# Four seams of a four-layer kernel: squares and projection by image in layer 0, a LayerNorm by token rows in layer 2, and the start and end of layer 3's attention

## The chip, the cores and the metric

The kernel runs on one core of one Trainium2 chip. The metric is the device time of one execution in microseconds. Before the change it was 3514.43 us, the median of 3 runs (3514.23 to 3514.61).

The core has five engines that run their own instruction streams beside each other: TensorE (PE in the profile, its weight loads are PEld), VectorE (DVE), ScalarE (ACT), GpSimd (POOL) and SyncE (SP, which here only issues DMAs). A matrix product goes from SBUF to PSUM; the other engines bring it back.

## The reference

Four layers follow one another on x, four images of 256 channels and 32 x 32 places (B = 4, D = 256, L = 1024 tokens per image). Cut to what matters:

```
# layer 0: a state space layer (Mamba-2) and a squeeze-and-excite gate
u = layernorm(x over channels)
y = scan(u) * silu(z)
y = y * rsqrt(mean(y * y) + eps) * rms_w          # per token
out = y @ out_w.T
attn = sigmoid(relu(mean_over_tokens(out) @ se1_w.T + se1_b) @ se2_w.T + se2_b)
x = x + out * attn                                  # one gate per image and channel
# layer 1: a non-local block, theta, phi and g with one channel each
f = theta x phi / N;  y = f @ g
x = x + batchnorm(w * y + b)
# layer 2: attention and a mixture of 8 experts, top 2, on t = tokens of x
n = layernorm(t);  t = t + softmax(q(n) k(n) / 16) v(n)
t = t + moe(layernorm(t))
# layer 3: attention over channels and an LSTM
n = layernorm(t);  query, key = n @ W_qk + b_qk;  value = n @ W_v + b_v
lam = softmax(key over tokens).T @ value            # 256 x 256 per image
lam = batchnorm(lam over images and value channels) * gamma + beta
t = t + query @ lam
t = t + lstm(layernorm(t))                          # 1024 steps, in order
```

All of it is in fp32.

## The kernel before, in words

The activations stay in SBUF. `s.x` holds x with the channels on the partitions (two chunks of 128 channels, C = 2), `s.xr` holds token rows (128 tokens on the partitions, 32 such tiles, NT = 32, 8 per image). A block is 512 tokens (W), of which an image has two (BPI = 2). A planner orders instructions on each engine by their dependencies, the order in which they are written and the buffers of the tile pools; a pool with n buffers makes the n+1st user wait for the first to be done. Where `_in_order` is called, the order written is fixed for PE, DVE and ACT.

Layer 0 ends with `_scan` (L376 to L436) and `_out_and_se` (L439 to L493). The scan goes over 8 chunks of 128 tokens of 4 images, 32 in all. `_out_and_se` first takes the 32 Squares with a sum on ACT (L449), a Sqrt on ACT (L451) and a reciprocal (L452). Then it goes over the eight blocks: the rows are scaled on DVE (L459), turned by PE (`pt`, L463), copied with rms_w on DVE (`yT`, L464) and projected (`po`, L470); ACT copies the result to `o` with a sum over tokens (L473). After the last block come the mean, the two small products of the gate, the sigmoid (L491) and eight updates of x on DVE (L493).

Layer 1 (`_layer1`, L499 to L612) reduces the block to sums: 64 matmuls (L535), one row of statistics, a chain of small DVE operations with `_rsqrt`, and then per image and channel chunk `theta` on PE (L602), `wy` on ACT (L607) and an addition to x on DVE (L612).

`_rsqrt` (L971 to L994) is a Newton iteration on DVE with four rounds; it is a generator, so that its operations can be placed beside other work.

Layer 2 begins with `_layernorm` (L184 to L216) for all eight blocks: the mean over channels by a matmul with a matrix of averages (L196), a subtraction on DVE (L197), Square on ACT (L199), the variance by a matmul (L201), and after the last block Sqrt (L209), reciprocal (L211), a broadcast by matmuls from eight rows (`wide`, L215) and the multiplication (L216). `_layer2_attention` (L712) then goes over the images: q (L743), v (L755), scores (L768) for eight groups of 128 queries with softmax between, the transposes of the probabilities (L792) and the product with v (L804). `beside(n)` takes n parts of a generator between these steps; for images 1 to 3 the parts are those of `_head` (the LayerNorm, gate and scatter for the experts) for the image before, for image 0 there are none. The experts follow; they scatter their results to DRAM from POOL's queue.

Layer 3's attention (`_layer3_attention`, L1247 to L1398) loads y, the two expert results of each token, by 16 DMAs from SP's queue (L1282), adds the two on POOL (L1285) and the sum to the token rows on DVE (L1287), takes statistics per tile of 128 tokens (L1291, L1292), then `_rsqrt` for the image's eight tiles, the normalised rows on ACT (L1302) and transposes (L1268, `p_x`) with copies on DVE (L1273). Keys (L1318), their softmax over tokens, and `lam` follow per image. After the last image comes the batch norm over all images (`_batchnorm`, L615, with a Sqrt on ACT, L625, and L1377, L1378). The query weights are folded into lam: `lam_q` by 16 matmuls (`p_q`, L1384), and the query bias by 32 (`p_b`, L1394) into `add_col`.

Layer 3's LSTM (`_layer3_lstm`) loads its weights on ACT's DMA queue, makes its constants (bias, `fold`, `mask`, `shift`, L1429 to L1443) and then `ahead(0)`: the attention output of the first 128 tokens of each image is added to x (`attended`, L1464 and L1458) and their input gates are computed (`input_gates`). The loop of 1024 steps takes one part of `ahead(n + 1)` per step beside its own chain: `hidden` on PE (L1616), transposes on DVE (L1645), activations on ACT (L1646, L1659), the new hidden state on DVE (L1661). The loop's order is fixed by `_in_order`.

Of the kernel before, what the change touches and what calls it, by code (L numbers as in the profile page):

```python
# [18 lines left out]
P = 128  # L19
B = 4  # L20
# [46 lines left out]
NW = {"w_l0": 260 + 512 + 256 + 64, "w_l2": 768 + 8, "w_l3": 768, "w_u": 768, "w_v": 768}  # L67
# [91 lines left out]
def _in_order(s, start):  # L159


    engines = mybir.EngineType
    before = {}
    for i in s.nc.cur_bb.bb.instructions[start:]:
        if i.engine not in (engines.PE, engines.DVE, engines.Activation):
            continue
# [17 lines left out]
def _layernorm(s, u):  # L184

    nc = s.nc
    with ExitStack() as ctx:
        pool = ctx.enter_context(s.tc.tile_pool(name="ln", bufs=2))
        ps = ctx.enter_context(s.tc.tile_pool(name="ln_ps", bufs=2, space=PSUM))
        ps1 = ctx.enter_context(s.tc.tile_pool(name="ln_ps1", bufs=1, space=PSUM))  # L190
        var = ps1.tile([NBLK, W], F32, name="var")
        for i in range(NBLK):
            t = bass.ts(i, W)
            mean = ps.tile([P, W], F32, name="mean")
            for k in range(C):
                nc.tensor.matmul(mean, s.avg, s.xt[:, k, t], start=k == 0, stop=k == C - 1)  # L196
            nc.vector.tensor_sub(u[:, :, t], s.xt[:, :, t], _bc(mean, 1, C))  # L197
            sq = pool.tile([P, C, W], F32, name="sq")
            nc.scalar.activation(sq, u[:, :, t], AF.Square)  # L199
            for k in range(C):  # L200
                nc.tensor.matmul(  # L201
                    var,
                    s.avg_row[:, NBLK - 1 - i : 2 * NBLK - 1 - i],
                    sq[:, k, :],
                    start=i == 0 and k == 0,
                    stop=i == NBLK - 1 and k == C - 1,
                )
        std = pool.tile([NBLK, W], F32, name="std", bufs=1)
        nc.scalar.activation(std, var, AF.Sqrt, bias=s.eps[:NBLK])  # L209
        rstd = pool.tile([NBLK, W], F32, name="rstd", bufs=1)  # L210
        nc.vector.reciprocal(rstd, std)  # L211
        for i in range(NBLK):
            t = bass.ts(i, W)
# [117 lines left out]
def _decays(s, keep, dtr):  # L331
# [41 lines left out]
    return dt, (a, head), total, tail  # L373


def _scan(s, xbc, zs, dt, decay, total, tail):  # L376

    nc, tc = s.nc, s.tc
    a, head = decay
# [1384 lines left out]
```

## Time and profile before

| What | Value |
|---|---|
| Runs | 3514.23 to 3514.61 us, median 3514.43 |
| Profiled execution | 3514.67 us |
| Its span | 3512.7 us (1.97 us lie around it) |
| Mean granted TensorE clock | 0.969 |
| PE, DVE, ACT, POOL busy in the span | 92%, 57%, 35%, 12% |
| Layer 0 to the end of the scan | 0 to 295.4 us |
| Projection and gate | to 358.9 us |
| Layer 1, first to last `theta` and x | to 394.6 us |
| LayerNorm of layer 2 | 393.4 to 442.4 us |
| Attention of layer 2, images 0 to 3 | from 442.4, 527.4, 615.2 and 701.9 us |
| Last scatter of the experts | issued at 1386.6 us |
| Attention of layer 3 | PE from 1423.0 to 1528.6 us |
| LSTM with its first inputs | from 1547 us to the end |

How to read the profile's lines: times are in us from the start of the span, L12 is line 12 of the kernel. A timeline line has the start, the duration of a run of equal instructions, the engine, the line, the operation, "out<-in" by the program's names, the shape and the count, and in brackets the time that the engine had been idle before it and what ended the idle time. The chain that ended last is followed back from the last instruction, at each step to what released it; "issue" there is time in which an engine waited for nothing that the profile shows. PEclk is the clock that TensorE was granted, 1.00 or a 9 in the slices for full speed. PE's ends are modelled, since its matmuls are pipelined.

### The profile page before, as it was taken

Reading aid. Unit: us, or ns where it says so; the run is one execution under the profiler, and the core shown is the slowest. Engines: PE = TensorE matmul, PEld = TensorE weight load, DVE = VectorE, ACT = ScalarE, POOL = GpSimd, SP = SyncE. Lnnn points to the kernel's source line nnn. Section 1 sums busy time; section 2 is a strip of 40 time slices with the busy share of each in tenths; the row PEclk is TensorE's granted clock in tenths of the full one; section 3 lists DMA queues with packets and bytes.
Section 4 is the critical chain, followed back from the end, with each engine's and each line's share of the span. In section 5 each row is a group of like instructions: output and inputs, shape, how many; then the busy total and the mean of one; then the engine's idle time right before and its main releaser. Section 6 shows DMA issues by size and latency. Waiting matters only on the chain.

```text
span 3512.7 us, 146893 instructions
## 1 busy us (share of the span) xinstructions
PE 3227.6 (92%) x65412; PEld 2536.4 (72%) x65412; DVE 2016.5 (57%) x8382; ACT 1245.0 (35%) x5047; POOL 416.3 (12%) x498
## 2 busy tenths in 40 slices
PE   7786899998999997789999999999999999999888
PEld 4464344447788886468888888888888888888776
DVE  5795534452211111747777776777777777767666
ACT  4623222223222222413334344343343343433333
POOL 0182001122433332100000000000000000000000
PEclk9898899999999999899999999999999999999999
DMA  1290001115556554100000000000000000000000
GB/s 67 80 303 5 9 0 37 37 50 197 195 189 219 208 190 165 60 2 4 4 11 4 5 10 4 4 10 4 6 9 5 10 4 5 10 4 5 10 4 10
DMA packets 79355, 189.31 MB, mean 54 GB/s; under 512 B 6592, under 2 KB 64256, under 8 KB 73728
## 3 DMA queue, kind: packets, MB, share of 16 engines
q0 software_dynamic: 16176, 116.06, 9.0%
q1 hardware_dynamic: 60624, 59.12, 5.7%
q8 instruction: 511, 8.37, 1.0%
q10 hardware_dynamic: 1920, 4.74, 0.4%
q14 instruction: 124, 1.02, 0.1%
HBM read 118.88 MB, written 61.02 MB: 51 GB/s over the span
## 4 chain that ended last, share of the span: by engine, by line
PE 41%; DVE 9%; ACT 4%; issue 2%; ACTq 0%; DVEq 0%
PE p_c L1616 11%; DVE turned L1645 7%; PE p_c L1607 7%; PE p_i L1607 4%; PE p_o L1607 4%; PE p_i L1616 4%; PE p_o L1616 4%; PE beside L1560 4%; ACT a_o L1646 2%; DVE x L1661 2%; ACT th L1659 2%; PE beside L1464 1%; PE beside L1501 0%; PE var L1511 0%; PE p_q L1384 0%
## 5 line engine op out<-in xcount | busy, mean ns | idle before, releaser
L1646 ACT ACTIVATE add<-turned 128x8 f32<-128x8 f32 x1024 | 214.3, 209 | 1027.5 <-DVE turned L1645 1027.5
L1616 PE MATMUL p_c<-w_v,x 128*4 128x64 f32 x16368 | 416.0, 219 | 72.8 <-DVE x L1661 71.0
L1607 PE MATMUL p_c<-xg,shift 128*128 128x64 f32 x2048 | 445.7, 299 | 0.0
L1616 PE MATMUL p_o<-w_v,x 128*4 128x64 f32 x16368 | 416.6, 219 | 0.1
L1616 PE MATMUL p_i<-w_v,x 128*4 128x64 f32 x16368 | 416.5, 219 | 0.0
L1607 PE MATMUL p_i<-xg,shift 128*128 128x64 f32 x2048 | 406.8, 280 | 0.0
L1645 DVE STREAM_TRANSPOSE turned<-p_c 128x64 f32<-128x64 f32 x1024 | 255.9, 250 | 257.1 <-PE p_c L1616 226.7
L1607 PE MATMUL p_o<-xg,shift 128*128 128x64 f32 x2048 | 396.0, 275 | 0.0
L1607 PEld LDWEIGHTS p_c<-xg,shift 128*128 128x128 f32 x2048 | 304.7, 188 | 117.6 <-issue 0.3
L1616 PEld LDWEIGHTS p_c<-w_v,x 128*4 128x4 f32 x16368 | 227.2, 85 | 196.3 <-DVE x L1661 121.2
L1661 DVE TENSOR_TENSOR x<-a_o,th 128x8 f32<-128x8 f32 x1024 | 171.9, 168 | 245.4 <-ACT th L1659 245.4
L1607 PEld LDWEIGHTS p_o<-xg,shift 128*128 128x128 f32 x2048 | 310.9, 192 | 0.3
L1607 PEld LDWEIGHTS p_i<-xg,shift 128*128 128x128 f32 x2048 | 304.8, 188 | 0.4 <-issue 0.3
L1187 PE MATMUL ph<-uT,w 128*128 128x256 f32 x1248 | 284.6, 386 | 20.8 <-DVE uT L1172 20.7
L1191 ACT ACTIVATE hT<-ph,w 128x256 f32<-128x256 f32 x312 | 147.9, 474 | 395.2 <-PE ph L1187 394.8
L1187 PEld LDWEIGHTS ph<-uT,w 128*128 128x128 f32 x1248 | 240.4, 194 | 58.2 <-DVE uT L1172 24.6
L1201 PE MATMUL po<-w,hT 128*128 128x256 f32 x1248 | 282.1, 379 | 0.0
L1616 PEld LDWEIGHTS p_o<-w_v,x 128*4 128x4 f32 x16368 | 281.2, 87 | 0.3 <-issue 0.3
L1616 PEld LDWEIGHTS p_i<-w_v,x 128*4 128x4 f32 x16368 | 281.2, 87 | 0.3
L1645 DVE STREAM_TRANSPOSE turned<-p_i 128x64 f32<-128x64 f32 x1024 | 271.6, 265 | 0.7 <-PE p_i L1607 0.3
L1645 DVE STREAM_TRANSPOSE turned<-p_o 128x64 f32<-128x64 f32 x1024 | 256.0, 250 | 0.3 <-PE p_o L1616 0.3
L1201 PEld LDWEIGHTS po<-w,hT 128*128 128x128 f32 x1248 | 234.0, 190 | 30.2
(437 smaller groups left out, 4395.4 us busy)
## 6 DMA issues: line engine op xcount, KB each, us to landing
sorted<-zeros SPq DMA_DIRECT2D x32, 1032.0 KB, 14.4
y_in<-results SPq DMA_DIRECT2D x16, 512.0 KB, 5.3
x<-in_x_dram SPq DMA_DIRECT2D x8, 512.0 KB, 8.7
tokens<-rows SPq DMA_DIRECT2D x4, 1024.0 KB, 4.7
x<-tokens SPq DMA_DIRECT2D x8, 512.0 KB, 4.2
out_dram<-x_l SPq DMA_DIRECT2D x64, 64.0 KB, 1.7
results<-y,place POOLq DMA_INDIRECT x78, 4.4
w_l<-in_w_l_dram ACTq DMA_DIRECT2D x1, 1092.0 KB, 11.4
```

Source lines behind the costliest of these rows:

```text
L1187: nc.tensor.matmul(ph, w1[:, k, bass.ts(n, P)], uT[:, k, :], start=k == 0, stop=k == C - 1,)
L1191: nc.scalar.activation(hT[:, n, :], ph, AF.Gelu, bias=b1[:, n : n + 1])
L1201: nc.tensor.matmul(po, hT[:, n, bass.ts(a, P)], w2[:, n, :], start=n == 0, stop=n == NHC - 1,)
L1464: nc.tensor.matmul(p, lam[:, k, b, bass.ts(m, P)], u_l3[:, k, b * L + n * SB : b * L + (n + 1) * SB], start=k == 0, stop=k == C - 1,)
L1560: nc.tensor.matmul(p[bass.ts(i, R), :], rows[:, k, bass.ts(g, R)], w_u[:, k, at : at + GQ // GC], start=k == 0, stop=k == C - 1, tile_posi ...
L1607: nc.tensor.matmul(p[:, :H], shift[:, row * B : row * B + P], xg[n][:, g, bass.ts(i, H)], start=True, stop=t == 0,)
L1616: nc.tensor.matmul(p[R * i : R * i + B, :H], hs[:, t - 1, bass.ts(k, B)], w_v[:, k, i * GQ + g * H : i * GQ + (g + 1) * H], start=False, s ...
L1645: nc.vector.transpose(zt.rearrange("p c w -> p (c w)"), pz[g][:, :H])
L1646: nc.scalar.activation(dst.rearrange("p (c b) -> p c b", c=C), zt[:, :, :B], f)
L1659: nc.scalar.activation(th, cell[:, :, 1], AF.Tanh)
L1661: nc.vector.tensor_mul(h, a_o, th)
```

## The change

Layer 0. Each chunk's Square goes into `_scan`, behind the chunk's last operation. `_out_and_se` takes 1/sqrt by `_rsqrt` on DVE, in two parts (28 columns and the last 4), so Sqrt and reciprocal go. It then goes over images, not blocks: scaling is shared by DVE and ACT, the copies out of the transposes are on ACT with the sums over tokens, rms_w is multiplied into the weights once (`wo`), the gate's means are taken from the projection's input (a product with the mean of the rows in place of the mean of the products), and the four products of an image stay in four PSUM banks until the gate of this image is there; PE's order within an image is written out. x is updated from PSUM, four operations per image.

Layers 1 and 2. `_layer1` is called from `_layer2_attention` between the loading of layer 2's weights and `_layer2_weights`. `_layernorm` is replaced by `_norm_parts` for one image: transposes of x to token rows, a copy on ACT and statistics on DVE, `_rsqrt`, the normalised rows on ACT, transposes back and copies on DVE. Image 0's parts are run in layer 1 after image 0's x is done, with DVE's order fixed from there to the end of image 1; those of images 1 to 3 are the parts beside image 0's attention. `theta` has one PSUM buffer and not two.

`_rsqrt` and the LSTM's copy of it have three rounds, not four.

Layer 3. The two y are added on DVE, one after the other, and POOL has none of it. Image 0 is normalised in two groups of 512 tokens, each with its own `_rsqrt`, in a fixed order; the additions of later images are held behind the last copy of image 0's normalised rows. The LSTM's constants and bias loads come ahead of the attention. The weight array has another 256 columns, the query weights in their other orientation: the queries of the first 128 tokens of each image are computed in the attention (`q`), so that the first block's output is `lam` times q, and folding the weights into `lam` (`queries`) becomes eight groups placed between the parts of `ahead(0)`. A Sqrt with no other use is put ahead of the batch norm, and the batch norm's two wide operations per chunk become one.

The diff, cut to its core:

```diff
-def _layernorm(s, u):
+def _norm_parts(s, pool, u, b, psum):
+    mv = pool.tile([P, TPI, 2], F32, name="mv")
+    rows = pool.tile([P, TPI, D], F32, name="rows")
+    for n in range(0, TPI, 2):
+        p = psum()
+        for i in range(2):
             for k in range(C):
+                at = i * D + k * P
+                nc.tensor.transpose(
+                    p[:, at : at + P], s.x[:, k, b, bass.ts(n + i, P)], s.ident
                 )
+        yield
+        nc.scalar.copy(rows[:, n : n + 2, :].rearrange("p n d -> p (n d)"), p)
+        stats = pool.tile([P, 2, nc.vector.BN_STATS_DIM], F32, name="stats")
+        for i in range(2):
+            nc.vector.bn_stats(stats[:, i, :], p[:, bass.ts(i, D)])
+        for i in range(2):
+            nc.vector.bn_aggr(mv[:, n + i, :], stats[:, i, :])
+        yield
+    rstd = pool.tile([P, TPI], F32, name="rstd")
+    for i, _ in enumerate(_rsqrt(s, pool, rstd, mv[:, :, 1])):
+        if i % 2:
+            yield
+    shift = pool.tile([P, TPI], F32, name="shift")
+    nc.vector.scalar_tensor_tensor(shift, mv[:, :, 0], -1.0, rstd, ALU.mult, ALU.mult)
+    yield
+    for n in range(TPI):
+        nc.scalar.activation(
+            rows[:, n, :], rows[:, n, :], AF.Identity,
+            bias=shift[:, n : n + 1], scale=rstd[:, n : n + 1],
+        )
+        if n % 4 == 3:
+            yield
+    for i in range(BPI):
+        for c in range(C):
+            p = psum()
+            for j in range(TPB):
+                nc.tensor.transpose(
+                    p[:, bass.ts(j, P)], rows[:, i * TPB + j, bass.ts(c, P)], s.ident
+                )
+            yield
+            nc.vector.tensor_copy(u[:, c, b * L + i * W : b * L + (i + 1) * W], p)
+            yield
...
 def _scan(s, xbc, zs, ss, dt, decay, total, tail):
...
+                sq = pool.tile([P, D], F32, name="sq")
+                nc.scalar.activation(sq, zs[:, n, :], AF.Square, accum_out=ss[:, c * B + b : c * B + b + 1])
...
 def _out_and_se(s, y, ss, w_out, w_se1, se2):
-        for n in range(NT):
-            sq = pool.tile([P, D], F32, name="sq")
-            nc.scalar.activation(sq, y[:, n, :], AF.Square, accum_out=ss[:, n : n + 1])
-        nc.scalar.activation(rstd, ss, AF.Sqrt, bias=s.eps, scale=1.0 / D)
-        nc.vector.reciprocal(rstd, rstd)
+        for t in (slice(0, NT - B), slice(NT - B, NT)):
+            nc.vector.tensor_scalar_mul(ms[:, t], ss[:, t], 1.0 / D)
+            for _ in _rsqrt(s, pool, rstd[:, t], ms[:, t]):
+                pass
+        for b in range(B):
...
+            start = len(nc.cur_bb.bb.instructions)
+            project(0, 0)
...
+            project(0, 1)
...
+            project(1, 0)
...
+            project(1, 1)
+            _in_order(s, start, (mybir.EngineType.PE,))
...
 def _layer1(s, first):
-        wide = ctx.enter_context(tc.tile_pool(name="l1_wide", bufs=2, space=PSUM))
+        wide = ctx.enter_context(tc.tile_pool(name="l1_wide", bufs=1, space=PSUM))
...
                 nc.vector.tensor_add(xs, xs, wy)
+            if b == 0:
+                start = len(nc.cur_bb.bb.instructions)
+                first(lambda: ps.tile([P, W], F32, name="p"))
+            elif b == 1:
+                _in_order(s, start, (mybir.EngineType.DVE,))
...
 def _layer2_attention(s, m):
-                _layernorm(s, u)
+                def first(psum):
+                    for _ in _norm_parts(s, norm, u, 0, psum):
+                        pass
+
+                _layer1(s, first)
                 _layer2_weights(s, w, keep, w_ps)
...
-            parts = _head(s, m, b - 1, psum) if b > 0 else iter(())
+            if b > 0:
+                parts = _head(s, m, b - 1, psum)
+            else:
+                parts = chain(*(_norm_parts(s, norm, u, i, psum) for i in range(1, B)))
...
-    for _ in range(4):
+    for _ in range(3):
...
 def _layer3_attention(s, x, u, lam, q):
-                    nc.gpsimd.tensor_add(y[:, 0], y[:, 0], y[:, 1])
-                    nc.vector.tensor_add(xr, xr, y[:, 0])
+                    for k in range(2):
+                        later(nc.vector.tensor_add(xr, xr, y[:, k]))
...
+                    if b == 0:
+                        normalise(g * TPB, TPB)
+                if b == 0:
+                    _in_order(s, start)
+                else:
+                    normalise(0, TPI)
...
+            nc.scalar.activation(pool.tile([P, C], F32, name="none"), total, AF.Sqrt)
...
-            nc.vector.tensor_scalar(v, v, mean, scale, ALU.subtract, ALU.mult)
-            nc.vector.tensor_scalar_add(v, v, s.col["beta"][:, m : m + 1])
-        for m in range(C):
-            for i in range(B * D // W):
...
-                        p, wq[:, k, bass.ts(m, P)],
-                        lam[:, k, bs, :].rearrange("p b d -> p (b d)"),
...
+            off = pool.tile([P, 1], F32, name="off")
+            nc.vector.tensor_mul(off, mean, scale)
+            nc.vector.tensor_sub(off, s.col["beta"][:, m : m + 1], off)
+            nc.vector.tensor_scalar(v, v, scale, off, ALU.mult, ALU.add)
...
 def _layer3_lstm(s, x, u_l3, lam, q, wq, constants):
-        for _ in ahead(0):
-            pass
+        start = len(nc.cur_bb.bb.instructions)
+        fill = queries()
+        first = 2 * C * B + 1
+        smalls = 0
+        for i, part in enumerate(ahead(0)):
+            smalls += bool(part)
+            if i in range(first + 1, first + 11, 2) or part and smalls % 4 == 1:
+                if next(fill, True) is None:
+                    end = len(nc.cur_bb.bb.instructions)
+        _in_order(s, start, (mybir.EngineType.PE,), end)
```

## The prediction

> **What bounds the kernel now.** I read the page's slices and its chain first, then the timeline of each stretch that the diff touches, engine by engine, then busy time by stretch with the granted clock.
>
> From the page of the kernel before (span 3512.7 us): TensorE's busy tenths and granted clock in 40 slices of 88 us, and the chain by engine.
>
> ```profile
> PE   7786899998999997789999999999999999999888
> PEclk9898899999999999899999999999999999999999
> ...
> PE 41%; DVE 9%; ACT 4%; issue 2%; ACTq 0%; DVEq 0%
> ```
>
> The right 22 slices are the LSTM: 1024 steps from 1583 to about 3507 us, 1.88 us each. Its PE order is unchanged; only three DVE instructions per block of steps go, out of parts that already fit. So 55% of the span stays, and what can move are four seams before it. Timeline of PE at these (start, duration, instruction, idle before and its releaser):
>
> ```profile
> 310.96 2.02 PE L463 MATMUL pt<-ident,zs 128*128 128x128 f32 x8 [16.98 <-DVE zs L459]
> 358.90 13.79 PE L535 MATMUL p<-x,w 128*32 128x512 f32 x64 [1.03 <-DVE x L493]
> 393.35 4.56 PE L196 MATMUL mean<-x,avg 128*128 128x512 f32 x10 [3.13 <-ACT wy L607]
> 427.02 14.01 PE L215 MATMUL wide<-rstd,spread 8*128 8x512 f32 x16 [4.14 <-DVE rstd L211]
> 442.44 9.12 PE L743 MATMUL p_mm<-u,mat 128*128 128x512 f32 x16 [1.41 <-DVE u L216]
> ...
> 527.43 7.03 PE L743 MATMUL p_mm<-u,mat 128*128 128x512 f32 x16
> ...
> 615.18 7.03 PE L743 MATMUL p_mm<-u,mat 128*128 128x512 f32 x16
> ```
>
> PE stands 17 us before the output projection; the LayerNorm's matmuls fill 393 to 442, and attention cannot start before. The last three lines are the first q of images 0, 1 and 2 (image 3's is at 701.89): an image takes 85.0, 87.8, 86.7 us. Timeline of ACT and DVE in the first two seams:
>
> ```profile
> 295.54 0.42 ACT L449 ACTIVATE sq<-zs 128x256 f32<-128x256 f32 x1 [7.44 <-DVE zs L436]
> 308.42 1.28 ACT L451 ACT_TABLE_LOAD   x1
> 310.46 1.93 DVE L459 TENSOR_SCALAR zs<-zs,rstd 128x256 f32<-128x256 f32 x7
> 382.27 2.30 ACT L607 ACTIVATE wy<-theta,off,coef 128x1024 f32<-128x1024 f32 x2 [10.54 <-DVE off L597]
> 423.63 3.34 DVE L211 RECIPROCAL rstd<-std 8x512 f32<-8x512 f32 x1 [3.83 <-ACT std L209]
> ```
>
> Layer 3's start and end, timeline of all engines:
>
> ```profile
> 1400.03 2.34 POOL L1285 TENSOR_TENSOR y_in<-y_in 128x1024 f32<-128x1024 f32 x1 [12.49 <-DMA y_in<-results]
> 1410.57 2.31 DVE L984 TENSOR_SCALAR rstd<-half 128x8 int32<-128x8 int32 x1
> 1423.03 2.17 PE L1268 MATMUL p_x<-ident,rows 128*128 128x128 f32 x8 [37.58 <-ACT rows L1302]
> 1530.48 1.28 ACT L625 ACT_TABLE_LOAD   x1 [14.57 <-issue]
> 1534.24 9.34 PE L1384 MATMUL p_q<-lam,w_l 128*128 128x512 f32 x16 [5.65 <-DVE lam L1378]
> 1543.43 3.63 PE L1394 MATMUL p_b<-cols,lam 128*128 128x1 f32 x32
> ```
>
> A DVE operation on 128x8, 0.17 us elsewhere, takes 2.31 while POOL adds y.
>
> **Part by part** (minus is a gain).
>
> **Layer 0's squares.** From the last zs (295.4) to the first scaling (310.46) are 15 us: 32 Squares at 0.40, a table load 1.28, Sqrt, reciprocal. Moved into the scan, they lie in ACT's idle time: ACT is busy 39.2 of 137 us there, 3 us free in each 4.29-us step, and the instruction order has each Square two or three chunks behind its data. Four stay after the scan (1.6), then a Newton chain on DVE, 14 dependent operations spaced 0.195 (L990 to L994 run 377.54 to 378.12): 2.7. First scaling at about 300.2: **-10** (-8 if the 28-column and 4-column chains run one after the other, -12 if the Squares end with the scan).
>
> **Projection by image.** Before: 310.5 to 358.9, 48.4 us, of which 5 are the squeeze tail. After, an image has 16 transposes (2.1), 16 matmuls (7.3), and PE waits some 2 for the last copy and the mean before its fixed order goes on: 11.3, times 4, plus 3 for the last sigmoid and x update: 48.2. **0** (-5 to +6). Behind this wait stand the next image's transposes.
>
> **LayerNorm of layer 2.** Before, from the first wy (382.27) to the first q (442.44): 60.2. After: wy 2.3 and an add 1.2 (+3.6); four pairs of statistics, each 2 x 0.41 + 2 x 0.16 on DVE beside the next transposes (+9.7 with the adds around them); Newton and shift 2.7 (+12.4); eight rows on ACT, 4.05 as at L1302 (+16.5); transposes and copies out (+18.4). But PE's order puts image 3's theta matmuls ahead of q, and theta now has one PSUM buffer, not two: they wait for wy of image 2 (2.3), that for a wy buffer, that for image 1's adds (2.36), which DVE has behind the norm: 18.4 + 4.6 = +23. **-37** (-42 if that queue costs nothing, -30 if rows and wy also queue on ACT).
>
> **Images 1 to 3 beside image 0's attention.** 75 parts in 88 slots, one image after another, since the norm's rows have one buffer. PE gets 96 transposes at 0.11 (8 in 1.04 less the pipelined end): 10.6; its idle time there is 5 of 85. DVE gets some 29 us on top of 30 (an image: statistics 4.2, Newton 2.7, copies out 2.8), ACT 19 on top of 18 (copies 2.4, rows 4.05). Cheapest case: the expert head beside images 1 to 3 adds 1 to 3 us (85.0 to 87.8 and 86.7) for 4.5 of PE work; by that, +5. Against it, PE's order ends with the last norm's 16 transposes ahead of the second value product, so its rows and copies (about 9) stand in the open: 10.6 + 9 = **+19**. Dearest, all three chains so: +30.
>
> What clock PE gets with many short waits, a stretch of the LayerNorm shows; busy time by stretch (length, PE, PEld, DVE, ACT, POOL with counts, granted clock, DMA share, GB/s):
>
> ```profile
> 404.00:427.00 23.00, 18.13 (x41) 4.43 (x39) 9.45 (x6) 8.15 (x8) 0.00 (x0) 0.98 0.00 0
> 427.00:442.00 15.00, 14.01 (x16) 4.31 (x16) 9.47 (x8) 0.00 (x0) 0.00 (x0) 0.50 0.00 0
> ```
>
> 79% busy got 0.98; only the broadcast matmuls from 8 rows, which go, ran at 0.50. Image 0 would be 87% busy (90.6 of 104): I take full clock. The Trainium skill, "TensorE: Matmul & The Clock Gate", section on psum-queue depth-cycling, speaks against the change: short idles between matmul groups make the clock swing between half and full. If half of image 0's 90 us of matmul fell to half clock, it would cost about 45 us and bring the sum to about 3510.
>
> **Layer 3's start.** y lands at 1400.0. Before, POOL add, DVE add, statistics, Newton (stretched by three stalls of 2.2) and rows reach PE at 1423. After: two adds 2.46, four statistics 2.1, Newton on four columns 2.8, first row 0.5: PE at 1408. The second half follows by 7.5 us of DVE, so image 0's keys end some 11 earlier; later images' adds are held behind its last copy, hidden under 23.7 us of PE per image (1457.06 to 1481.03). On ACT's DMA queue w_l (1024 columns for 768) and four b_l loads (0.44 each to issue, at 1547 before) go ahead of w_u and w_v, after the last scatter; SP's 16 y loads keep their order, POOL loses its 16 adds. w_u and w_v land off y or beside it: the bounds hold both. **-11** (-16 to -5).
>
> **Layer 3's end.** Off the chain: p_q and p_b (12.7), the Sqrt load (1.2 of 1.28), constants on DVE (1.6, 1547.17 to 1548.73), one Newton round (0.6). Added: four matmul groups for q (1.7). The eight query groups (10.5 of PE) return among the first block's inputs, where PE idles 5.5 of 34: I take 5 in the open. -16.1 + 6.7 = **-9.4** (-14 all hidden, -4 all open).
>
> Three Sqrt loads leave the path at 1.28; in the row at 1530.48 the activation follows after 0.02. The Trainium skill, "ScalarE: Activation LUTs", section on what a table load costs, adds a drain for 2.66 in all; by that the sum is 4 lower, about 3461.
>
> **Newton with three rounds, not four:** layers 0 and 1, three operations at 0.195 each: **-1**.
>
> **Sum**: -10 + 0 - 37 + 19 - 11 - 9.4 - 1 = -49.4. The profiled run took 3514.67 (span 3512.7 and 1.97 around it), 0.24 over the median of 3514.43. 3514.43 - 49.4 = **3465**.
>
> **Rivals** (times worked out from the sum).
> First, **The cover holds better**: image 0 costs +5, theta's queue nothing: -19 more, 3446. For it: the head's small price. Against: the order at the end of image 0.
> Second, **The norm is given back in image 0**: three chains of 16 us (+3.6 to +18.4 above) in series instead of 19: +29, 3494. For it: two PSUM buffers shared with v and the value product. Against: eleven slots per step spread the parts.
> Third, **Layer 3's seams don't move** because y lands late and the queries stay open: +16, 3481. For it: 37 us of PE idle hang on one transfer. Against: DVE's stalls beside POOL are seen, not inferred.
> Fourth, **Slower**: a Square that stands in ACT's queue ahead of the exponential of the next chunk's mask and waits for DVE lengthens every scan step. Price 32 times the wait: from 49 / 32 = 1.5 us per step it eats everything; at 2 us the time is 3465 + 64 = 3529. Against: 3 us of slack per step and an order two chunks late.
>
> **How the numbers follow.** Forecast 0.64 (3450 to 3482), rival 1 0.13, rival 2 0.12, rival 3 0.06, rival 4 0.05. The range 3441 to 3493 takes in rivals 1 and 3 and nearly rival 2; outside stay about 0.17. 0.2% (7 us) is what can be told from no change: faster 0.94, same 0.02, slower 0.04.
>
> **What would show it.** Squares between 160 and 295; first transposes of zs near 300; layer 1's matmuls near 349; first q 23 us after the first wy; image 0's attention 104 us with DVE releasing PE; PE in layer 3 starting 15 us sooner after the last scatter, with no POOL adds; after lam no 128x512 query matmuls, and the first LSTM step some 9 us sooner after lam. I am wrong if attention of image 0 exceeds 125 us or runs at a lower clock, the scan grows by over 5 us, or a step leaves 1.88.

## The result and the profile after

The changed kernel takes 3462.33 us (median of 4 runs, 3459.98 to 3464.93) against 3514.33 us (median of 4, 3510.33 to 3514.61): a ratio of 0.9855, 95% interval 0.9838 to 0.9872. It is faster by 52 us. The forecast was 3465. The profiled execution took 3464.93, the slowest of the four; its span is 3463.2, which is 49.5 less than before.

From the page of the changed kernel: span, TensorE's busy tenths and granted clock in 40 slices, the chain by engine.

```profile
span 3463.2 us, 147312 instructions
...
PE   7788799989899997899999999999999999999888
...
PEclk9899899999999998999999999999999999999999
...
PE 44%; DVE 10%; ACT 4%; issue 2%; DMA 0%; ACTq 0%; SPq 0%; DVEq 0%
```

The picture is the old one, a little shorter: the LSTM still fills the right half. The seams are read in the timeline. TensorE around layers 0 to 2 of the changed kernel (start, duration, instruction, idle before and its releaser):

```profile
297.40 3.65 PE L496 MATMUL pt<-ident,zs 128*128 128x128 f32 x16 [5.61 <-ACT zs L490]
...
345.48 7.07 PE L592 MATMUL p<-x,w 128*32 128x512 f32 x64 [1.48 <-DVE w L570]
...
384.48 3.78 PE L659 MATMUL theta<-rows,spread 128*128 128x512 f32 x4 [4.69 <-ACT wy L664]
390.65 8.83 PE L814 MATMUL p_mm<-u,mat 128*128 128x512 f32 x16 [2.39 <-ACT wy L664]
...
473.24 2.16 PE L226 MATMUL p_mm<-ident,rows 128*128 128x128 f32 x8 [5.07 <-ACT rows L216]
...
493.30 7.03 PE L814 MATMUL p_mm<-u,mat 128*128 128x512 f32 x16
...
581.30 7.03 PE L814 MATMUL p_mm<-u,mat 128*128 128x512 f32 x16
```

PE stands 5.6 us and not 17.0 before the output projection; layer 1's 64 matmuls take 7.07 and not 13.79; the LayerNorm's own matmuls are gone, and q of image 0 starts at 390.65 and not at 442.44. It waits for a wy of layer 1 (the addend of x that layer 1 computes). Image 0's attention lasts 102.7 (390.65 to 493.30) for 85.0 before, with a PE gap of 5.07 near its end.

Layer 3's attention on TensorE, changed kernel:

```profile
1371.36 2.17 PE L1365 MATMUL p_x<-ident,rows 128*128 128x128 f32 x8 [20.97 <-ACT rows L1399]
1374.22 3.75 PE L1440 MATMUL p_mm<-u_l,w_l 128*128 128x512 f32 x4 [0.69 <-issue]
...
1382.17 6.88 PE L1440 MATMUL p_mm<-u_l,w_l 128*128 128x512 f32 x12 [0.68 <-DVE u_l L1369]
...
1410.66 1.92 PE L1365 MATMUL p_x<-ident,rows 128*128 128x128 f32 x8 [1.28 <-ACT rows L1399]
...
1490.40 3.70 PE L1496 MATMUL p_mm<-u_l,w_l 128*128 128x512 f32 x8
1495.68 4.18 PE L1597 MATMUL beside<-q,lam 128*128 128x128 f32 x30 [1.04 <-DVE lam L1515]
```

The last scatter is issued at 1351.52, so the first transposes come 19.8 us behind it (36.5 before). But image 1's come only at 1410.66. At the end the matmuls for q (1490.40) lie beside the batch norm, and lam times q follows at once.

Stretch by stretch, each from one instruction to the next one named, in us of the two profiled executions:

| Stretch | Before | After | Difference | Predicted |
|---|---|---|---|---|
| Start to first matmul of the scan | 161.54 | 159.49 | -2.05 | part of -1 |
| Scan, to the last zs | 133.46 | 133.61 | +0.15 | 0 |
| Last zs to first scaling | 15.46 | 3.80 | -11.66 | -10 |
| First scaling to layer 1's first matmul | 48.44 | 48.58 | +0.14 | 0 |
| Layer 1's first matmul to first wy | 23.37 | 16.58 | -6.79 | part of -1 |
| First wy to first q | 60.17 | 28.59 | -31.58 | -37 |
| Image 0, q to q | 84.99 | 102.65 | +17.66 | +19 |
| Image 1's q to last scatter | 859.15 | 858.22 | -0.93 | 0 |
| Last scatter to last lam (ahead of its batch norm) | 141.62 | 138.34 | -3.28 | -11 |
| Last lam to the LSTM's first recurrent matmul | 54.74 | 44.54 | -10.20 | -9.4 |
| From there to the end | 1929.76 | 1928.80 | -0.96 | 0 |
| Sum | | | -49.50 | -49.4 |

The sum agrees to 0.1 us, and three of its terms do not; how far two executions of the same code differ in these stretches is said with the experiments' table. Layer 1 gave 6 us that the prediction did not see, and the LayerNorm's stretch and layer 3's start gave 5 and 8 us less than it said. The experiments ask about these first.

### The profile page after: what moved, and what is told of

Its sections match the earlier page's. It is cut to its first block, busy times and chain, and to the rows that moved or that the text cites. A ratio compares the mean times of both kernels' runs of the same rounds, so it can differ in the third digit from the quotient of the medians.

```text
span 3463.2 us, 147312 instructions
## 1 busy us (share of the span) xinstructions
PE 3212.0 (93%) x65540; PEld 2545.9 (74%) x65540; DVE 2009.5 (58%) x8480; ACT 1267.9 (37%) x5119; POOL 399.0 (12%) x490
## 3 DMA queue, kind: packets, MB, share of 16 engines
q14 instruction: 125, 1.02, 0.1%
## 4 chain that ended last, share of the span: by engine, by line
PE 44%; DVE 10%; ACT 4%; issue 2%; DMA 0%; ACTq 0%; SPq 0%; DVEq 0%
PE p_c L1747 11%; DVE turned L1786 7%; PE p_c L1738 7%; PE p_i L1738 5%; PE p_o L1747 4%; PE p_o L1738 4%; PE p_i L1747 4%; PE beside L1691 4%; ACT a_o L1787 2%; DVE x L1802 2%; ACT th L1800 2%; PE p_u L1469 1%; PE beside L1597 1%; PE p_mm L1440 1%; PE beside L1632 1%
## 6 DMA issues: line engine op xcount, KB each, us to landing
w_l<-in_w_l_dram ACTq DMA_DIRECT2D x1, 1092.0 KB, 11.7
```

## The experiments

The kernels below are run once each, with a profile, except the last. Between single executions the same code of layer 2's later images and the experts (image 1's q to the last scatter) took from 855.5 to 863.9 us, so whole spans can't be compared to a few us; the kernel before took 3515.95 to 3519.94 us in its single runs beside these. Stretches can be compared, some better than others. Where a run left a stretch's code as it is in the changed kernel, image 0 took 102.4 to 103.7 us, last scatter to lam 136.2 to 139.6, and last lam to the first recurrent matmul 42.9 to 47.4. The first is known to about 1 us, layer 3's two stretches only to some 3 and 5; by that the gain of 3.28 at layer 3's start may be anything from near 0 to 5.4. This table has those that the edits touch; "wy to q" is first wy to first q, "images 0 and 1" are q to q, "scatter to lam" is layer 3's attention.

| Kernel | zs to scaling | Layer 1 | wy to q | Image 0 | Image 1 | Scatter to lam | Span |
|---|---|---|---|---|---|---|---|
| before | 15.46 | 23.37 | 60.17 | 84.99 | 87.75 | 141.62 | 3512.7 |
| changed | 3.80 | 16.58 | 28.59 | 102.65 | 88.00 | 138.34 | 3463.2 |
| layer 0 alone | 4.47 | 16.65 | 61.90 | 84.92 | 87.71 | 139.76 | 3494.3 |
| Squares after | 15.99 | 16.59 | 28.17 | 102.36 | 87.85 | 139.59 | 3473.9 |
| four rounds | 4.47 | 17.17 | 29.06 | 98.52 | 87.42 | 141.20 | 3470.7 |
| norm whole | 3.80 | 16.59 | 62.69 | 85.02 | 88.03 | 136.27 | 3481.4 |
| wy ahead | 3.80 | 16.59 | 24.57 | 106.74 | 87.97 | 138.85 | 3465.3 |
| more parts per step | 3.80 | 16.58 | 28.61 | 103.89 | 87.15 | 138.34 | 3461.5 |
| one y | 3.80 | 16.58 | 28.45 | 103.72 | 86.86 | 133.12 | 3455.5 |
| no hold | 3.79 | 16.58 | 28.49 | 102.44 | 87.89 | 138.78 | 3466.5 |
| third norm beside image 1 | 3.80 | 16.59 | 28.46 | 88.43 | 92.09 | 136.22 | 3453.7 |
| wy ahead, held in u | 3.80 | 16.59 | 24.53 | 100.40 | 87.73 | 137.24 | 3457.9 |
| keys copied by ACT | 3.81 | 16.59 | 28.60 | 102.64 | 88.00 | 132.28 | 3459.5 |
| three edits together | 3.79 | 16.59 | 23.22 | 86.75 | 92.09 | 132.88 | 3438.3 |

### Layer 0's part alone

```diff
 # the kernel before, with these two functions of the change and nothing else
-        _scan(s, xbc, zs, dt, decay, total, tail)
-        _out_and_se(s, zs, w_out, w_se1, se2)
+        ss = keep.tile([P, NT], F32, name="ss")
+        _scan(s, xbc, zs, ss, dt, decay, total, tail)
+        _out_and_se(s, zs, ss, w_out, w_se1, se2)
```

> The kernel before with layer 0's two parts alone (Squares in the scan, projection by image); Newton keeps four rounds and layers 1 to 3 stay. Theory: layer 1's 64 matmuls took 13.79 us before only because they waited for the eight updates of x on DVE (357.5 to 367.1), which the projection by image does earlier; so first layer-1 matmul to first wy falls from 23.4 to about 17, last zs to first scaling from 15.5 to about 4.4 (one round more than in the changed kernel), and the span by about 17, to 3496. Rival: layer 1 became shorter through its own edits (PSUM pools, the weights' operations moved, one Newton round less); then it stays at 23 here and the span falls by 11 only, to 3502.

Layer 1 fell to 16.65 without any edit of its own, the span to 3494.3. So the 6.8 us that layer 1 gained belong to layer 0's edit. How this looked before, on ACT, PEld and DVE of the kernel before, and on PE and ACT with layer 0's part alone:

```profile
368.31 0.69 ACT L539 ACTIVATE rows<-p,bias 128x512 f32<-128x512 f32 x1 [10.14 <-PE p L535]
...
367.18 0.14 PEld L535 LDWEIGHTS p<-x,w 128*32 128x32 f32 x2 [0.20 <-DVE x L493]
...
357.47 9.66 DVE L493 SCALAR_TENSOR_TENSOR x<-o,att,x 128x1024 f32<-128x1024 f32 x8 [0.71 <-ACT att L491]
```

```profile
346.59 7.07 PE L577 MATMUL p<-x,w 128*32 128x512 f32 x64
...
348.66 0.69 ACT L581 ACTIVATE rows<-p,bias 128x512 f32<-128x512 f32 x1 [3.41 <-PE p L577]
```

Before, the matmuls that the first copy (`rows`) needs were through only at 368.3, 9.4 us after the first began and 1.2 after the last of the eight updates of x (367.1); with the part alone they are through after 2.1. TensorE also had only half its clock there, 0.50 from 358.9 to 364.6, but that did not set the end: from 364.6 to 372.7 it had 1.00, and the weight loads still waited for x, the last at 367.18. The timeline shows PE busy for 13.79 us without a break in the first case. A run of matmuls that is far longer than its count allows (64 take 7.07) is waiting, though the row says busy. The releaser that the row names, x at L493, is the one to look at.

### The Squares back behind the scan

```diff
-                sq = pool.tile([P, D], F32, name="sq")
-                nc.scalar.activation(sq, zs[:, n, :], AF.Square, accum_out=ss[:, c * B + b : c * B + b + 1])
...
+        for n in range(NT):
+            b, c = divmod(n, TPI)
+            sq = pool.tile([P, D], F32, name="sq")
+            nc.scalar.activation(sq, y[:, n, :], AF.Square, accum_out=ss[:, c * B + b : c * B + b + 1])
```

> The changed kernel with the 32 Squares back behind the scan, all else as changed. Theory: last zs to first scaling grows from 3.8 to about 15 (28 more Squares at 0.40), the scan stays at 133.6, the span grows by 11 to 3474. Rival: the Squares inside the scan cost it something; then the scan gets shorter by that and the span grows by less than 9.

15.99 for 3.80, span 3473.9. In the changed kernel ACT does the Squares like this at the end of the scan:

```profile
290.14 0.42 ACT L455 ACTIVATE sq<-zs 128x256 f32<-128x256 f32 x1 [2.16 <-DVE zs L453]
...
293.61 0.42 ACT L455 ACTIVATE sq<-zs 128x256 f32<-128x256 f32 x1 [2.96 <-DVE ms L479]
...
296.90 1.71 ACT L490 ACTIVATE zs<-zs,rstd 128x256 f32<-128x256 f32 x4 [2.78 <-DVE rstd L1065]
```

Each Square follows its own zs, by 0.03 to 0.64 us over all 32, and only one is left behind the last zs (which ends at 293.52). The scan takes 132.6 without the Squares and 131.8 to 133.8 with them in the other runs: they cost nothing there that can be seen. The rival by which a Square delays the scan (the one that would have made the kernel slower) is out.

### Four Newton rounds again

```diff
-    for _ in range(3):
+    for _ in range(4):
```

> The changed kernel with four Newton rounds again. Theory: a round is three dependent operations at 0.195 to 0.2 and lies on the path in the four norms of layer 0's front (2.05 us in the comparison of the two traces), once each in layer 0's end, layer 1, the norm of image 0, the last norm beside image 0, layer 3's two groups and the LSTM's first inputs: some 10 times 0.6, span +6, 3469. Rival, as in the prediction: only 1.6 of it shows, 3465.

The span grew by 7.5, but 4.1 of this is image 1's q to the last scatter (862.3 for 858.2), which differs as much without any edit. Layer 0's front grew by 2.6 (scan start at 162.12), its end by 0.67, layer 1 by 0.59, the norm of image 0 by 0.47. Layer 3's attention took 2.9 more, of which 1.6 lies above the 136.2 to 139.6 of the other runs. The prediction's 1 us for this was too small; the norms of layer 0 stand in a row, four times 0.6. What nobody expected: image 0's attention became shorter by 4.1, though each of its three norms had three operations more.

### The LayerNorm whole, as before

```diff
-                _layer1(s, first)
+                _layer1(s, lambda psum: None)
+                _layernorm(s, u)
                 _layer2_weights(s, w, keep, w_ps)
...
-            if b > 0:
-                parts = _head(s, m, b - 1, psum)
-            else:
-                parts = chain(*(_norm_parts(s, norm, u, i, psum) for i in range(1, B)))
+            parts = _head(s, m, b - 1, psum) if b > 0 else iter(())
```

> The changed kernel with the LayerNorm of layer 2 over all images as before, after layer 1, and no parts beside image 0's attention. Theory: first wy to first q goes from 28.6 back to about 60, image 0's attention from 102.7 back to 85, the span grows by 14 to 3477. Rival: part of the 31.6 us of that stage came from elsewhere (layer 1 done earlier, weights' operations moved out); then the stage comes back to 55 or less and the span grows by under 9.

62.69 and 85.02: by this comparison the norm by token rows is worth 34.1 us and costs 17.6 in image 0, net 16.5. The stretch's gain is the norm's own and does not come from layer 1.

### theta and wy ahead of the norm

The chain ahead of q in the changed kernel, on ACT and DVE:

```profile
382.13 2.30 ACT L664 ACTIVATE wy<-theta,off,coef 128x1024 f32<-128x1024 f32 x2 [3.08 <-DVE x L669]
388.30 2.30 ACT L664 ACTIVATE wy<-theta,off,coef 128x1024 f32<-128x1024 f32 x2 [3.87 <-PE theta L659]
...
379.62 1.29 DVE L230 COPY u<-p 128x512 f32<-128x512 f32 x2 [0.82 <-PE p L226]
380.82 2.35 DVE L669 TENSOR_TENSOR x<-x,wy 128x1024 f32<-128x1024 f32 x2
```

u of image 0 is ready at 380.9. Then image 1's additions free a wy buffer, wy of image 2 runs (382.13), theta of image 3 (384.48), wy of image 3 (388.30), and q starts 0.05 after that (390.65): 9.7 us between u and q.

```diff
-                wy = pool.tile([P, L], F32, name="wy")
+                wy = pool.tile([P, L], F32, name="wy", bufs=8)
...
-                xs = s.x[:, c, b, :]
-                nc.vector.tensor_add(xs, xs, wy)
+                held.append((s.x[:, c, b, :], wy))
             if b == 0:
-                start = len(nc.cur_bb.bb.instructions)
-                first(lambda: ps.tile([P, W], F32, name="p"))
-            elif b == 1:
-                _in_order(s, start, (mybir.EngineType.DVE,))
+                for xs, wy in held:
+                    nc.vector.tensor_add(xs, xs, wy)
+                held = []
+        start = len(nc.cur_bb.bb.instructions)
+        first(lambda: ps.tile([P, W], F32, name="p"))
+        for xs, wy in held:
+            nc.vector.tensor_add(xs, xs, wy)
+        _in_order(s, start, (mybir.EngineType.DVE,))
```

> The changed kernel, but theta and wy of images 1 to 3 are issued ahead of image 0's norm (eight wy buffers for two) and their additions to x behind it. Theory: q of image 0 waits until wy of image 3 has read its PSUM, and that waits for the wy buffers, for image 1's additions and for the norm on DVE; with the buffers it does not, and first wy to first q falls from 28.6 to about 20, the span by 8 to 3455. Rival: ACT's queue (norm rows behind six wy of 1.15 us) takes the place; then 26 or more and the span falls by 3 at most.

q came 4.0 earlier and the second q not at all (131.3 from wy to second q, 131.2 before the edit). Neither expectation held. In this run, on PE, ACT and DVE:

```profile
385.78 3.70 PE L818 MATMUL p_mm<-u,mat 128*128 128x512 f32 x8 [1.27 <-DVE u L230]
393.36 5.40 PE L818 MATMUL p_mm<-u,mat 128*128 128x512 f32 x8 [3.88 <-ACT q L823]
...
392.62 1.27 ACT L823 ACTIVATE q<-p_mm,r 128x512 f32<-128x512 f32 x2 [8.67 <-issue]
...
385.64 6.89 DVE L677 TENSOR_TENSOR x<-x,wy 128x1024 f32<-128x1024 f32 x6
```

q's first copy begins 0.1 us after the last addition of wy ends (385.64 + 6.89 = 392.53), after ACT had stood 8.7 us, though its product needs only some 2 us from 385.78 (in the next run 386.33 to 388.40). The two share no data, and the copy's other input, `r`, was written at 358.2; what they share is SBUF, since q's buffer was given out where layer 1's pools had been. "issue" in the bracket means that the profile shows no wait, so that the cause is so far only argued; the next run asks.

### wy ahead, held in u

```diff
-                wy = pool.tile([P, L], F32, name="wy", bufs=8)
+                wy = pool.tile([P, L], F32, name="wy") if b == 0 else u[:, c, bass.ts(b, L)]
```

> As the run with theta and wy of images 1 to 3 ahead of the norm, but wy of these images is written into the part of u that their own norm fills later, so that no SBUF of layer 1 is still being read when attention begins. In the run before, q's matmuls began 24.6 us after the first wy but q's first copy waited until the last addition of wy (392.5), because q's SBUF had been layer 1's. Theory: that wait is the rest; the second group of q no longer waits 3.9, and first wy to second q (131.2 in the changed kernel, 131.3 in the run before) falls to about 126. Rival: the norms beside image 0 set its end whatever q does; then it stays within 1.5 of 131.2.

```profile
386.33 7.13 PE L818 MATMUL p_mm<-u,mat 128*128 128x512 f32 x16 [1.27 <-DVE u L230]
...
388.40 0.69 ACT L823 ACTIVATE q<-p_mm,r 128x512 f32<-128x512 f32 x1 [3.91 <-PE p_mm L818]
```

PE's and ACT's rows of this run: the copy of q now waits for its product alone, the 16 matmuls run without a break, and wy to second q is 124.9, 6.3 less than in the changed kernel. The additions of wy ended no sooner here (386.19 + 6.89 = 393.08), and q's copy no longer waits for them. Only the place of wy differs between the two runs, so the wait on layer 1's SBUF was the rest.

### More parts per step beside image 0

```diff
-                for _ in range(n):
+                for _ in range(n + 2 if b == 0 else n):
                     next(parts, None)
```

> The changed kernel with 17 and not 11 parts per step beside image 0's attention, so that the three norms are issued earlier. Theory: of the 17.7 us that image 0 grew by, some 8 are the last norm's chain in the open (PE idle 5.07, 0.98, 0.66 and slow transposes between 465 and 478); issued earlier it lies beside scores and value products, and image 0 falls from 102.7 to about 96. Rival: DVE's and PE's added work is the bound, or the two PSUM buffers shared with the value product; then image 0 stays within 2 us of 102.7.

103.89: nothing gained. The gap moved, it did not close. PE was busy 3.83 of the 10 us from 450 to 460 in this run, with a wait of 4.78 for ACT's rows, and the gap from 465 to 479 was gone: the third norm now stood ahead of the first value product instead of the second. DVE was busy 8.73 of these 10 us. By the runs so far this left the rival standing.

### The third norm beside image 1

```diff
-            if b > 0:
-                parts = _head(s, m, b - 1, psum)
-            else:
-                parts = chain(*(_norm_parts(s, norm, u, i, psum) for i in range(1, B)))
+            norms = [_norm_parts(s, norm, u, i, psum) for i in ((1, 2), (3,), (), ())[b]]
+            parts = chain(*norms, *([_head(s, m, b - 1, psum)] if b > 0 else []))
...
-                for _ in range(n):
+                for _ in range(n + 1 if b == 1 else n):
```

> The changed kernel with the norms of images 1 and 2 beside image 0's attention and that of image 3 beside image 1's, ahead of the expert head there (one part more per place). Theory: image 0 grew by 17.7 us for two reasons, the transposes on PE (10.6 in all) and the third norm's chain, which meets the value products (PE idle or at half clock between 465 and 479); without the third norm image 0 falls from 102.7 to about 91, image 1 grows from 88.0 by 4 to 5, the two together fall by 6. Rival: wherever the third norm stands it costs the same; then the two together stay within 2 us of 190.7.

88.43 and 92.09, together 10.1 less than in the changed kernel. Busy time by stretch (length, PE, PEld, DVE, ACT, POOL with counts, granted clock, DMA share, GB/s), first the changed kernel, then this one:

```profile
400.00:448.00 48.00, 46.71 (x194) 27.49 (x193) 35.88 (x114) 22.69 (x42) 0.00 (x0) 1.00 0.00 1
461.00:470.00 9.00, 5.93 (x45) 4.64 (x43) 7.78 (x23) 3.38 (x6) 0.00 (x0) 1.00 0.01 2
470.00:479.00 9.00, 4.74 (x17) 3.19 (x18) 4.66 (x18) 4.04 (x8) 0.00 (x0) 0.52 0.00 0
```

```profile
398.00:445.00 47.00, 45.72 (x191) 27.00 (x189) 34.96 (x113) 21.68 (x40) 0.00 (x0) 1.00 0.00 1
457.00:466.00 9.00, 8.32 (x41) 5.20 (x40) 3.87 (x6) 1.17 (x2) 0.00 (x0) 1.00 0.01 2
466.00:477.00 11.00, 11.00 (x27) 4.79 (x26) 0.69 (x1) 0.00 (x0) 0.00 (x0) 1.00 0.00 0
```

The first two norms are hidden: PE is 97% busy at full clock in the first 48 us. The third meets the value products: its chain stands in the open (PE 10.7 busy in 18 us), and from within the 5.07 us gap PE has half its clock (0.50 from 470.4 to 480.6). With it gone, two norms cost image 0 only 3.4 us (88.43 for 85.02), less than the 7.1 of their transposes by the prediction's price (10.6 for three), and the third costs image 1 4.1. In image 0 the same third norm cost 14.2 (102.65 less 88.43). That image 0 was 4.1 shorter with four rounds fits this: PE's two largest gaps in that stretch were then 2.33 and 1.02, not 5.07, and the third norm's parts stood in other places. That the extra operations moved them is not shown, and why just that order is better wasn't tried.

### One y for the later images

```diff
-                    for k in range(2):
+                    for k in range(2 if b == 0 else 1):
                         later(nc.vector.tensor_add(xr, xr, y[:, k]))
```

> The changed kernel without the addition of the second y for images 1 to 3 (left out, the loads stay). Theory: between image 0's keys (end at 1389.1) and image 1's transposes (1410.7) DVE is the bound, since it now does both additions; without six of them (7.4 us, about 4 of it before image 1's norm) image 1's first transposes come 4 us sooner, the image period goes back to 23.7, and image 3's keys start 5 sooner. Rival: PE's own order and image 0's softmax set image 1's start; then it moves by under 1.5 us.

This kernel leaves out a part of the result and serves for its times alone. Last scatter to lam fell by 5.2, 3.1 below the fastest of the runs whose layer 3 is that of the changed kernel. Image 1's first transposes came 3.3 sooner behind the last scatter (55.9 for 59.1), where 4 was expected, its keys ended 5.4 sooner (67.3 for 72.7), and image 3's keys started 5.3 sooner (108.2 for 113.5): the whole gain is there by the end of image 1's keys. DVE's additions are on the path between image 0 and image 1.

### No hold

```diff
-                if ahead is not None:
+                if False:
                     tc.add_manual_dep(
```

> The changed kernel without the hold of later images' additions behind image 0's last copy. Theory: DVE's work is the same and only its order changes: image 0's keys come up to 4 us later, image 1's up to 4 sooner, image 3's keys within 1.5 us of 1465.0. Rival: the hold pushes 14 us of additions into image 0's softmax and so costs; then image 3's keys start 3 or more sooner.

Image 0's keys ended 47.4 behind the last scatter, not 37.5: 9.9 later, more than the 4 expected. Image 1's ended at 73.0 and not 72.7, image 3's began at 113.46 and not 113.51. The lead that the hold gives image 0 is real and is lost in full by image 1 already; the hold only moves work inside the stretch between the two.

### Turned keys copied by ACT

```diff
-                    nc.vector.tensor_copy(kt, p_k.rearrange("p m q -> p (m q)"))
+                    nc.scalar.copy(kt, p_k.rearrange("p m q -> p (m q)"))
```

> The changed kernel with the copies of the turned keys in layer 3 (eight per image, 0.38 each) on ACT instead of DVE. Theory: DVE bounds the images of layer 3's attention since it has both additions of y (without six of them, last scatter to lam fell from 138.3 to 133.1); 3 us less per image give last scatter to lam about 135. Rival: ACT's longer copies (0.48) lie in the chain of transpose, copy and product and cost what DVE gains; then 138 or more.

132.28, 6.1 less, where about 3 was expected, and 3.9 below the fastest of the runs whose layer 3 is that of the changed kernel. ACT's copies were not longer (0.375 for 0.42), as the rival had it. Busy time by stretch in the changed kernel, from the end of image 0's keys to image 1's transposes, and from the end of image 1's keys to image 2's:

```profile
1389.00:1410.60 21.60, 15.82 (x73) 11.73 (x71) 19.34 (x67) 5.94 (x12) 0.00 (x0) 0.92 0.45 147
...
1424.20:1441.06 16.86, 15.54 (x88) 12.47 (x87) 10.47 (x34) 10.02 (x22) 0.00 (x0) 1.00 0.00 1
```

In the first stretch DVE is busy 19.3 of 21.6 us, PE 15.8, ACT 5.9. Some 6 of the 19.3 are additions of y at 1.2 each, half of which POOL had before. In the second DVE is busy 10.5 of 16.9 and PE 15.5. So work taken off DVE pays in the first stretch and not in each image after it: in this run image 1's keys ended 5.3 sooner behind the last scatter (67.3 for 72.7), image 3's 5.1 (115.5 for 120.5), and from image 1 on the keys of an image ended 23.9 to 24.2 us behind those of the one before it, as they do in the changed kernel (23.9 and 24.0) and in the kernel before (24.0 and 23.7). Two experiments by different edits (one y, this one) gave 5.2 and 6.1: DVE bounds the stretch between image 0's and image 1's keys in the changed kernel. Why less than 4 us of copies were worth over 5 there isn't shown; between runs of the same code this stretch differs by 1.5.

### The three edits together

wy held in u, the third norm beside image 1, the keys copied by ACT.

> The changed kernel with the three edits together: wy of images 1 to 3 ahead of the norm and held in u, the third norm beside image 1, the turned keys copied by ACT. Theory: they act in different stretches, so they add up: first wy to third q from 219.2 to 203 (6.3 and 10.1 less), last scatter to lam from 138.3 to 132.3, in all 22 less than the changed kernel's 3462, 3440; against the kernel before a ratio of about 0.979. Rival: the first two share one cover (the norms' chain beside image 0) and do not add; then 3447.

3440.98 us (median of 5, 3437.78 to 3443.89) against 3510.19 (median of 9): a ratio of 0.9802, interval 0.9789 to 0.9816, which does not touch that of the changed kernel. First wy to third q is 202.1 (203 expected), last scatter to lam 132.9. They add up, as they act in different stretches. TensorE in this run:

```profile
382.31 7.13 PE L816 MATMUL p_mm<-u,mat 128*128 128x512 f32 x16 [1.19 <-DVE u L230]
...
469.06 7.03 PE L816 MATMUL p_mm<-u,mat 128*128 128x512 f32 x16
```

q waits for u alone (1.19), and image 0 takes 86.8 us with two norms beside it. This version beats both kernels.

## Why the prediction was right, and where its steps failed

The total was right, 49.4 forecast and 49.5 measured in the traces, and it was right partly by luck: 13 us of gain that it overrated (5.4 in the LayerNorm, 7.7 at layer 3's start) were made up for by 7.8 that it left out (layer 1 and the Newton rounds) and by 5.4 of small differences in the other rows of the table.

**Right as worked out, or nearly:**

- The Squares (-10, measured -11.7): ACT's idle time in the scan covers them as said, and one Newton chain is left (2.75 us, 294.15 to 296.90). But the order was not two or three chunks late: each Square ran right behind its data, and one and not four stood after the last zs, hence the 1.7 more.
- The projection by image (0, +0.14).
- Image 0 (+19, +17.7), and for the reason given: the last norm's chain in the open ahead of the second value product. The two terms of this sum were off in opposite directions, though: two norms beside image 0 cost 3.4 us where their transposes were priced at 7.1, and the third cost 14.2 where its own transposes and chain were priced at 3.5 + 9. The dearest case given for image 0, +30, does not follow from its terms either: 10.6 + 3 x 9 is 37.6.
- Layer 3's end (-9.4, -10.2): from the first product of lam to the first recurrent matmul it takes 40.2 us for 36.0 before, with one round less, so 4.8 of the queries' 10.5 us were open; 5 had been taken. That this agrees so well is in part luck: the same code took 38.5 to 43.1 in the other runs, at a granted clock of 1.00 to 0.88, which makes 3 to 8 us open.
- PE's clock: 1.00 over the 48 us of image 0 where short waits are many. There the rule of the Trainium skill ("TensorE: Matmul & The Clock Gate", psum-queue depth-cycling) did not show; in image 0 the clock fell to 0.50 only behind the two gaps over 1 us, 2.39 us just before q (391.9 to 395.3) and 5.07 (470.4 to 480.6).
- The Sqrt load: statistics to reciprocal went from 1.88 (1530.22 to 1532.10) to 0.55 (1491.89 to 1492.44), so this load is worth 1.3 as its row said, not the 2.66 of the skill's page on activation tables ("ScalarE: Activation LUTs").

**"Newton with three rounds: layers 0 and 1, -1."** Too small: with the round taken back, layer 0's front, its end, layer 1 and the norm of image 0 grew by 4.3 us together, seven rounds at about 0.6, and 2.6 of this in layer 0's front alone.

**"Projection by image: 0", with nothing for layer 1.** This is the step that failed by omission. The row of 13.79 us at L535 was quoted, and no gain was taken from it. It was waiting for x: 6.7 us of gain for layer 1 come with layer 0's part alone.

**"+23, the LayerNorm's -37."** The chain was seen (image 1's additions, wy, theta) but cut off one link too soon: theta of image 3 took 3.78 us (1.98 at full clock) and its wy 2.30, which had to read PSUM before q could have it. Measured 28.6: u was ready after 18.8, where 18.4 had been forecast, and the queue behind it took 9.7 and not 4.6. The bound given, -42 without that queue, would have needed one thing more, an SBUF of q's own: with the queue gone, q's copy waited for layer 1's SBUF, and only wy in u gave 6.3 of it back. Even then first wy to first q was 24.5 and not 18.4.

**"Layer 3's start, -11: later images' adds ... hidden under 23.7 us of PE per image."** Image 0's keys did end 11.7 sooner behind the last scatter (37.5 for 49.2). The clause that failed is the cover: DVE's own work between image 0 and image 1 was not added up. With the second addition of y it was busy 19.3 of 21.6 us there, image 1's keys ended only 4.8 sooner behind the last scatter (72.7 for 77.5), and 3.3 us were left at lam.

Of the rivals none came about. Rival 1 (the cover holds better) is near to what the three edits give for layer 2: 86.8 + 92.1 for images 0 and 1, 6.1 more than before. The wait of rival 4 did not come either (the scan took 0.15 us more), though the late order that was to speak against it is not what ran.

## What to carry to other kernels

Where work is moved beside other work, add up the busy time of the engine that takes it over the whole stretch, not only at the place where it starts; a lead won at the first item is given back at the next if that engine is full between the two. Where two runs of the same code differ by 3 us in a stretch, an edit there has to give more than that before it is believed. Where a row of equal instructions is longer than its count, look at its releaser before taking it for work. When a wait is removed, look at the memory: the next wait can be a buffer that two stages share by turns, and the profile may name nothing for it.

## What the runs showed of the hardware that was not expected

- A run of 64 matmuls was shown as 13.79 us busy, with a granted clock of 0.79, while it waited for its input in parts; the same 64 took 7.07 at 1.00.
- In the changed kernel a PE gap of 5.07 us (468.2 to 473.2) came with a granted clock of 0.50 from 470.4 to 480.6, and the value product's 32 matmuls, begun at 478.4, took 15.1 instead of the 13.9 of the run with the third norm beside image 1. Forty-eight us with PE 97% busy and many short waits had 1.00.
- The same code from lam's first product to the first recurrent matmul took 38.5 us where the granted clock was 1.00 in it (keys copied by ACT, more parts per step), 40.2 at 0.96 (the changed kernel) and 43.1 at 0.88 (no hold, the three edits together).
- Single executions of the same code of layer 2's later images and the experts differed by 8 us (855.5 to 863.9), more than most of the edits are worth; the cause is open.
